# Layer 1's lookup tables in two float32r parts, in a kernel of four graph layers

## The chip, the cores and the metric

The kernel runs on one core of one Trainium2 chip. The metric is the device time of one execution in microseconds (us).

## The reference

The input is x with 16 graphs of 1,024 nodes and 128 features, and adj, one 1,024 x 1,024 matrix of zeros and ones for each graph. Four layers follow each other, each with a residual and a layer norm:

```python
x = layernorm(x + L0(x))   # attention over adj: q, k, v with relu, softmax over neighbours
x = layernorm(x + L1(x))   # max over neighbours
x = layernorm(x + L2(x))   # (x + adj^T x) through two dense layers
x = layernorm(x + L3(x))   # three SAGE convolutions on a dilated graph, batch norm, dense
```

The change is in layer 1:

```python
p = einsum('bnd,do->bno', x, W1 - W2)
q = einsum('bnd,do->bno', x, W2)
pre = p[:, :, None, :] + q[:, None, :, :] + b
return max(relu(pre) * adj[..., None], axis=2)
```

Layer 3 first thins out the graph ("dilation"). It goes row by row through a matrix: a row's neighbours are counted, a part of them is removed by rank, and removals also take the mirrored column, so that later rows see them.

## The kernel before

**Layer 1.** Relu is monotone, so what is needed is the max of q[j, o] over the neighbours j of each row i. Seven columns j make a group, 147 groups a graph. For a chunk of 21 groups, VectorE (DVE) builds the maxima of all 128 subsets of a group's columns for every o (`sub`, L257, seven instructions). For three groups at a time TensorE (PE) transposes them into PSUM (`pt`, L264) and ScalarE (ACT) copies them to `table` (L266). For each group PE multiplies `lit` with the columns of adj (`pm`, L271, bf16, one PSUM buffer of its own with the tag `subset`), and ACT makes of it the one-hot subset of each row (`hot`, L273, two buffers). A float32 product of `table` and `hot` (`pg`, L148 in the helper `product`) looks the maxima up, into one of two PSUM buffers with the tag `wide`, which other layers share. DVE takes the running max (`best`, L249). The product of group g is issued behind the `pm` of group g + 1.

**What runs beside it.** The function `between` is called after every group. It puts in the layer 2 of the graph before (`gin`), the layer 0 of the graph after (`attention`, one tile of 128 rows every ten groups) and an even share of the dilation (`dilation`, 1,400 pieces for 2,352 groups).

**The dilation** works on 8 blocks of 128 rows, for all 16 graphs. Each block loads its rows as bytes (`E`, L327, one buffer, by POOL's queue) and the block's own corner (`Dg`). For each graph, `E` is cleared of what earlier blocks removed (L341) and counted by ACT (`junk`, L343 and L347). Then 127 steps follow, each a chain of ten small DVE instructions on 16 partitions (L361 to L374). The corner is written out and read back into `E` (L378 and L379), ACT counts it (`junk`, L383, 16 times), seven small DVE instructions make constants of the counts, and for each graph DVE ranks (`rank`, L400, one buffer), ACT takes an absolute value (L401) and DVE makes `gone` (L403), which SP's queue stores.

**The order.** Instructions are not issued in the order in which the code lists them. A scheduler places them on each engine, by priorities and by its own estimate of how long each takes, and fixes the order when the program is built. Each engine then runs its own list in that order and waits where a semaphore is not yet set. A change in layer 1 can therefore move other work.

**Layer 3** starts when layers 0 to 2 are done (L486 is its first large DVE instruction) and is the same in both kernels.

Of the kernel before, what the change touches and what calls it, by code (L numbers as in the profile page):

```python
"""Four graph layers with residuals and layer norms, on one NeuronCore.  # L1

Rows of a graph's features stand either on the partitions (x[n, d]) or in the free dimension  # L3
(xT[d, n]); adj is read both as it is and with its rows and columns swapped, in bfloat16, in which
its zeros and ones are exact.

Layer 0  masked attention, a tile of 128 query rows at a time.
Layer 1  max over neighbours of q[j, o]: relu is monotone, so relu(p + b + max q) is the max of
         relu(p + q + b), and a row without neighbours gives 0. Seven columns j make a group; the
         maxima of its 128 subsets are tabled for every o, and a matrix product with the one-hot  # L10
         subset of each row i (exact) looks them up. What is left is a max over the 147 groups.
Layer 2  GIN; x is split in three bfloat16 parts, whose sum is x, for the product with adj.
Layer 3  GraphSAGE on the dilated graph. Dilation goes row by row: in a block of 128 rows only the
         block's own 128 columns change while it is worked on, so they alone are stepped through,
         for 16 graphs at once on 16 partitions; the removals of whole rows follow in bulk. It
         depends on adj and nodemask alone and is issued between the groups of layer 1.
"""

# [8 lines left out]

F32 = mybir.dt.float32
BF = mybir.dt.bfloat16
U8 = mybir.dt.uint8  # L30
AF = mybir.ActivationFunctionType
ALU = mybir.AluOpType
# [3 lines left out]
B, N, D, H2 = 16, 1024, 128, 256  # L36
# [14 lines left out]
def subset_tables():  # L51
    """lit[j, g, s]: 1 or -1 for a column j of group g, in subset s or not; 1 - |s|."""
    s = np.arange(P)
    lit = np.zeros((CH, GC, P), np.float32)
    for j in range(CH):
        lit[j, j // GS] = np.where((s >> (j % GS)) & 1, 1.0, -1.0)
    size = sum((s >> k) & 1 for k in range(GS))
    return lit, (1.0 - size).astype(np.float32).reshape(P, 1)
# [3 lines left out]
def tile_graph_layers(ctx: ExitStack, tc, a, out):  # L62
# [14 lines left out]

# [1 line left out]
    ident = consts.tile([P, P], F32, name="ident")  # L79
# [38 lines left out]

    # Half of the mask: [b, n] and [p, t, b]; the whole in the latter form.
    mask_u = consts.tile([B, N], U8, name="mask_u")  # L120
    nc.sync.dma_start(out=mask_u, in_=a["nodemask"])
    half_mask = consts.tile([B, N], F32, name="half_mask")
    nc.vector.tensor_scalar(half_mask, mask_u, 0.5, None, op0=ALU.mult)
    nm = consts.tile([P, T, B], F32, name="nm")
# [10 lines left out]

# [1 line left out]
    def transposed(dst, src):  # L137
        """dst[d, n] from src[p, t, d], n = t * 128 + p."""
        for h in range(2):
            p = bank("ptr")  # L140
            for t in range(4):
                nc.tensor.transpose(p[:, t * P:(t + 1) * P], src[:, 4 * h + t, :], ident)
            nc.scalar.copy(dst[:, halves[h]], p)

    def product(lhsT, rhs, name):
        p = wide(name)
        for s in halves:
            nc.tensor.matmul(p[:, s], lhsT, rhs[:, s], start=True, stop=True)  # L148
        return p
# [14 lines left out]
    def split(pool, src, left):  # L164
        """Three bfloat16 tiles, the sum of which is src."""
        parts = [pool.tile([P, T, D], BF, name=f"part{k}") for k in range(3)]
        for k in range(3):
            nc.scalar.copy(parts[k], left if k else src)  # L168
            if k < 2:
                nc.vector.tensor_sub(left, left if k else src, parts[k])  # L170
        return parts

    def aggregate(parts, m, name):
        """[d, i]: the sum over j of x[j, d] m[j, i]."""
        p = wide(name)
        for s in halves:
            for c in range(T):
                for k in range(3):
                    nc.tensor.matmul(p[:, s], parts[k][:, c, :], m[:, c, s],  # L179
                                     start=(c == 0 and k == 0), stop=(c == T - 1 and k == 2))  # L180
        return p

    def layers_012():
# [4 lines left out]

# [1 line left out]
        def attention(b, An):  # L190
# [14 lines left out]
            for t in range(T):  # L205
# [3 lines left out]
                e = w4.tile([P, N], F32, name="e", bufs=2)  # L209
                # scores of relu'd q and k are not negative, and the mask is 0 or 1.  # L210
                nc.vector.scalar_tensor_tensor(e, psc, CLAMP_HI, An[:, t, :], op0=ALU.min, op1=ALU.mult)
# [21 lines left out]

# [1 line left out]
        def max_conv(b, AT, between):  # L235
# [7 lines left out]

            def look_up(g, table, hot):
                pg = product(table, hot, "pg")
                if g == 0:
                    nc.vector.tensor_copy(best, pg)
                else:
                    nc.vector.tensor_max(best, best, pg)  # L249

            last = None
            for g0 in range(0, NG, TG):
# [6 lines left out]
                for g in range(g0, g0 + TG):  # L259
                    at = (g - g0) % 3  # L260
                    if at == 0:
                        pt = bank("pt")
                        for k in range(3):
                            nc.tensor.transpose(pt[:, k * P:(k + 1) * P], sub[:, g - g0 + k, :], ident)  # L264
                        table = w2.tile([P, 3, P], F32, name="table", bufs=3)
                        nc.scalar.copy(table.rearrange("s g o -> s (g o)"), pt[:, :3 * P])  # L266
                    c, r = divmod(g, GC)
                    rows = min(CH, N - c * CH)
                    pm = wide("pm", "subset", 1)
                    for s in halves:  # L270
                        nc.tensor.matmul(pm[:, s], lit[:rows, r, :], AT[:rows, c, s], start=True, stop=True)  # L271
                    hot = w2.tile([P, N], F32, name="hot", bufs=2)
                    nc.scalar.activation(hot, pm, AF.Relu, bias=one_less)  # L273
                    if last is not None:
                        look_up(*last)
                    last = g, table[:, at, :], hot
                    between(g)
# [12 lines left out]

# [1 line left out]
        def gin(b, An):  # L292
# [26 lines left out]

# [1 line left out]
        # h1 = sf + 1 with sf = ceil(num / 2); half = num / 2 + 1/4 where the row is masked in,  # L321
        # 0 elsewhere: num > 10 where half > 5.5, num > 1 where half > 1.
        def dilation():
            for k in range(T):
# [4 lines left out]
                nc.gpsimd.dma_start(out=Dg, in_=adj[:, own, own])  # L329
                # Neighbours before and after the block's own columns.  # L330
                counts = dil.tile([P, 2, B], F32, name="counts")
# [25 lines left out]
                for n in range(P - 1):  # L357
                    mine = Dg[:, n, :]
                    m = slice(k * P + n, k * P + n + 1)
                    rank1 = small.tile([B, P], F32, name="rank1")  # L360
                    nc.vector.tensor_tensor_scan(rank1, mine, mine, before[:, n:n + 1], op0=ALU.add, op1=ALU.max)  # L361
# [7 lines left out]
                    nc.vector.tensor_scalar(at2, at, 2.0, -1.0, op0=ALU.mult, op1=ALU.add)  # L369
                    hit = small.tile([B, P], F32, name="hit")  # L370
                    nc.vector.tensor_scalar(hit, rank1, at, every, op0=ALU.is_equal, op1=ALU.max)  # L371
# [3 lines left out]
                    yield  # L375
                # Rows as each was when its turn came; what each removed.
                Dd = dram.tile([B, P, P], U8, name=f"own{k}")
# [3 lines left out]
                for b in range(B):  # L381
                    junk = dil.tile([P, N], BF, name="junk", tag="gone", bufs=2)
                    nc.scalar.activation(junk, E[:, b, :], AF.Copy, accum_out=num[:, b:b + 1])  # L383
                    yield
                # |scale * rank - centre| == width: both multiples of sf, the whole row, or none of it.
                half = dil.tile([P, B], F32, name="half")
# [35 lines left out]

        # Between the groups of a graph's layer 1: the last graph's layer 2, the next one's
        # layer 0 and an even share of the dilation.
        dilate = dilation()
# [38 lines left out]

# [1 line left out]
    xpool = ctx.enter_context(tc.tile_pool(name="xpool", bufs=1))  # L466
# [9 lines left out]
    def dilated(b):  # L476
        """[j, i], the edge from i to j that is left; kept for the later convolutions."""
        gone = sb.tile([P, T, N], BF, name="gone_all", bufs=1)
# [12 lines left out]
    def sage(b, l, m, hT, parts, stats):  # L491
# [23 lines left out]
        inv = sb.tile([P, N], F32, name="inv", bufs=1)  # L515
        # max(sqrt(s), 1e-12) = sqrt(max(s, 1e-24))
        nc.vector.tensor_scalar_max(inv, pn, 1e-24)  # L517
# [22 lines left out]
    def add_hidden(b, l, hT):  # L540
        """x += mask * (h_l @ Wl_l), with bl once."""
        p = wide("pl").rearrange("p (t d) -> p t d", d=D)
# [67 lines left out]
```

## Time and profile before

| What | Value |
|---|---|
| median of 3 runs | 9,834.1 us (9,832.8 to 9,841.0) |
| span of the profiled execution, first to last instruction | 9,842.3 us; the profile gives no other time for it |
| PE, DVE, ACT, POOL busy, share of the span | 85%, 81%, 44%, 5% |
| lookups `pg` on PE (two passes for each float32 product) | 9,408 matmuls, 4,516.5 us busy |
| `best` on DVE | 2,336, 1,213 ns each |
| `hot` on ACT | 2,352, 1,112 ns each |
| last `best` starts / layer 3's L486 starts | 7,957.6 / 8,038.5 us |
| mean granted TensorE clock | 0.926 |

The busy shares are averages over stages with different limits. In a row of the groups stand the line, the engine, the operation, what it writes and reads, shapes and count; behind the first bar its busy time and the mean duration of one, behind the second the idle time of the engine just before it and what ended most of that. In a row of the timeline stand the start and the duration in us, the engine, the line and the operation, and in brackets the idle time before it and its releaser. Matmuls are pipelined: four passes that follow each other show 1.88 us, and the distance from start to start is what one costs.

### The profile page before, as it was taken

What the parts mean: (1) busy time and instruction counts of PE and PEld (TensorE: products, weight loads), DVE (VectorE), ACT (ScalarE), POOL (GpSimd) and SP (SyncE); (2) the same over time, 40 slices, a digit from 0 to 9 for tenths busy, and PEclk for the clock granted to TensorE, in tenths of its full rate; (3) what the DMA queues carried; (4) which work ended last, traced back from release to release, by engine and by line L of the source; (5) the groups of instructions that cost most, each with busy time, mean ns of one, the idle gap of its engine ahead of it and who ended that gap; (6) DMA issues with size and microseconds to landing.
All of it is one profiled execution on the core that took longest, in us unless ns stands there. A gap on an engine that the chain in (4) does not pass through costs nothing. (4 is left out here: it accounts for less than half of the span.)

```text
span 9842.3 us, 86106 instructions
## 1 busy us (share of the span) xinstructions
PE 8394.1 (85%) x28929; PEld 4159.1 (42%) x29032; DVE 7991.7 (81%) x17348; ACT 4296.9 (44%) x5170; POOL 499.6 (5%) x447
## 2 busy tenths in 40 slices
PE   8888988898888888888889898989898967678775
PEld 4444444444444444444444444444444433344333
DVE  5998699869986998699869986998699968845556
ACT  4445544554455445544554455445444532122221
POOL 0000000000000000000000000000000001011111
PEclk9999999999999999999999999999999988889886
DMA  3010201020102010201020102010200047733332
GB/s 47 1 22 19 34 1 22 18 37 1 22 17 40 1 22 16 44 1 22 15 47 1 22 12 52 1 22 10 50 5 9 8 139 208 200 116 137 115 129 87
DMA packets 317235, 435.16 MB, mean 44 GB/s; under 512 B 105445, under 2 KB 156792, under 8 KB 316662
## 3 DMA queue, kind: packets, MB, share of 16 engines
q1 hardware_dynamic: 219696, 295.75, 9.1%
q0 software_dynamic: 92560, 132.72, 8.7%
q8 instruction: 227, 3.72, 0.2%
q10 hardware_dynamic: 4534, 1.19, 0.1%
q14 instruction: 218, 1.79, 0.1%
HBM read 461.64 MB, written 119.54 MB: 59 GB/s over the span
## 5 line engine op out<-in xcount | busy, mean ns | idle before, releaser
L148 PE MATMUL pg<-hot,table 128*128 128x512 f32 x9408 | 4516.5, 604 | 140.4 <-DVE best L249 83.0
L273 ACT ACTIVATE hot<-pm,one_less 128x1024 f32<-128x1024 f32 x2352 | 2616.1, 1112 | 2435.5 <-PE pm L271 2162.5
L249 DVE TENSOR_TENSOR best<-best,pg 128x1024 f32<-128x1024 f32 x2336 | 2833.9, 1213 | 465.4 <-PE pg L148 458.5
L148 PEld LDWEIGHTS pg<-hot,table 128*128 128x128 f32 x9408 | 1735.6, 191 | 1795.6 <-issue 1187.8
L271 PE MATMUL pm<-AT,lit 126*128 126x512 bf16 x4704 | 1428.1, 384 | 247.2 <-ACT hot L273 175.4
L271 PEld LDWEIGHTS <-lit 126*128 126x128 bf16 x4704 | 460.3, 99 | 1224.5 <-issue 1200.1
L266 ACT COPY table<-pt 128x384 f32<-128x384 f32 x784 | 371.5, 476 | 772.5 <-PE pt L264 763.8
L264 PE MATMUL pt<-ident,sub 128*128 128x128 f32 x2352 | 414.3, 284 | 179.4 <-DVE sub L257 99.8
L179 PE MATMUL pagg<-m,part 128*128 128x512 bf16 x2231 | 518.4, 383 | 36.8 <-DVE inv L517 25.3
L264 PEld LDWEIGHTS pt<-ident,sub 128*128 128x128 f32 x2352 | 305.1, 146 | 487.1 <-issue 244.3
L361 DVE TENSOR_TENSOR_SCAN rank<-Dg,before 16x128 f32<-16x128 uint8 x1016 | 477.6, 470 | 26.6
L179 PEld LDWEIGHTS <-part 128*128 128x128 bf16 x3072 | 298.5, 99 | 394.5 <-issue 55.0
L374 DVE TENSOR_TENSOR Dg<-Dg,hit 16x127 uint8<-16x127 uint8 (+63 forms) x1016 | 441.4, 434 | 22.9
L257 DVE TENSOR_TENSOR sub<-sub,q 128x21 f32<-128x21 f32 (+6 forms) x784 | 431.6, 550 | 15.7 <-ACT q L239 11.3
L208 POOL TENSOR_SCALAR pen<-An 128x1024 f32<-128x1024 bf16 x128 | 133.8, 1045 | 4639.8 <-DVE e L212 3004.0
L372 DVE SCALAR_TENSOR_TENSOR hit<-rank,sc,hit 16x128 f32<-16x128 f32 x1016 | 342.5, 337 | 25.0
L544 PE MATMUL pl<-w_L_gnn_Wl,hT 128*128 128x128 f32 x768 | 201.0, 369 | 181.0 <-DVE x L547 119.4
L168 ACT CAST part<-left 128x1024 bf16<-128x1024 f32 x128 | 133.6, 1044 | 490.4 <-DVE left L170 490.4
L226 PE MATMUL pav<-v,eT 128*128 128x128 f32 x2048 | 332.5, 329 | 12.9 <-ACT eT L223 12.5
L371 DVE TENSOR_SCALAR hit<-rank,sc 16x128 f32<-16x128 f32 x1016 | 336.9, 332 | 0.0
L226 PEld LDWEIGHTS pav<-v,eT 128*128 128x128 f32 x2048 | 309.8, 239 | 54.2 <-ACT eT L223 52.0
L519 DVE RECIPROCAL inv<-inv 128x1024 f32<-128x1024 f32 x48 | 314.3, 6549 | 19.1 <-ACT inv L518 19.0
(163 smaller groups left out, 8299.1 us busy)
## 6 DMA issues: line engine op xcount, KB each, us to landing
m<-kept SPq DMA_DIRECT2D x32, 2048.0 KB, 9.3
An<-in_adj_dram POOLq DMA_DIRECT2D x16, 2048.0 KB, 14.0
removed<-gone SPq DMA_DIRECT2D x128, 256.0 KB, 2.0
m<-in_adjT_dram POOLq DMA_DIRECT2D x16, 2048.0 KB, 13.5
gone_all<-removed SPq DMA_DIRECT2D x16, 2048.0 KB, 9.7
kept<-m SPq DMA_DIRECT2D x16, 2048.0 KB, 14.1
AT<-in_adjT_dram POOLq DMA_DIRECT2D x16, 2016.0 KB, 14.5
hidden<-r SPq DMA_DIRECT2D x48, 512.0 KB, 3.8
```

What stands on the lines that cost most here:

```text
L148: nc.tensor.matmul(p[:, s], lhsT, rhs[:, s], start=True, stop=True)
L179: nc.tensor.matmul(p[:, s], parts[k][:, c, :], m[:, c, s], start=(c == 0 and k == 0), stop=(c == T - 1 and k == 2))
L226: nc.tensor.matmul(pav[:, :D], eT[:, c, :], v[:, c, :], start=(c == 0), stop=(c == T - 1))
L249: nc.vector.tensor_max(best, best, pg)
L257: nc.vector.tensor_max(sub[:, :, n:2 * n], sub[:, :, 0:n], qg[:, g0:g0 + TG, k:k + 1].to_broadcast([P, TG, n]))
L264: nc.tensor.transpose(pt[:, k * P:(k + 1) * P], sub[:, g - g0 + k, :], ident)
L266: nc.scalar.copy(table.rearrange("s g o -> s (g o)"), pt[:, :3 * P])
L271: nc.tensor.matmul(pm[:, s], lit[:rows, r, :], AT[:rows, c, s], start=True, stop=True)
L273: nc.scalar.activation(hot, pm, AF.Relu, bias=one_less)
L361: nc.vector.tensor_tensor_scan(rank1, mine, mine, before[:, n:n + 1], op0=ALU.add, op1=ALU.max)
L372: nc.vector.scalar_tensor_tensor(hit, rank1, at2, hit, op0=ALU.is_equal, op1=ALU.max)
L374: nc.vector.tensor_tensor(Dg[:, n + 1:, n], Dg[:, n + 1:, n], hit[:, n + 1:], op=ALU.is_gt)
```

## The change

Each table is split in two. `high` is the transposed table written by ACT as float32r; `whole` is a second ACT copy in float32; `low`, their difference, is made on POOL as float32r. `hot` is written as float32r. The lookup of a group is two products for each half of the rows, with `high` and with `low`, added up in the same PSUM buffer. `high` and `low` have two buffers, `whole` one; `table` had three. Apart from that the mask is loaded by POOL's queue straight into float32, where SP's queue loaded bytes, and the small tiles `rank1` and `hit` of the dilation have two buffers in place of three. Comments are left out, so line numbers shift by up to eight.

```diff
+F32R = mybir.dt.float32r
...
-    mask_u = consts.tile([B, N], U8, name="mask_u")
-    nc.sync.dma_start(out=mask_u, in_=a["nodemask"])
     half_mask = consts.tile([B, N], F32, name="half_mask")
-    nc.vector.tensor_scalar(half_mask, mask_u, 0.5, None, op0=ALU.mult)
+    nc.gpsimd.dma_start(out=half_mask, in_=a["nodemask"])
+    nc.vector.tensor_scalar(half_mask, half_mask, 0.5, None, op0=ALU.mult)
...
-            def look_up(g, table, hot):
-                pg = product(table, hot, "pg")
+            def look_up(g, parts, hot):
+                pg = wide("pg")
+                for s in halves:
+                    for k, part in enumerate(parts):
+                        nc.tensor.matmul(pg[:, s], part, hot[:, s], start=(k == 0), stop=(k == 1))
...
-                        table = w2.tile([P, 3, P], F32, name="table", bufs=3)
-                        nc.scalar.copy(table.rearrange("s g o -> s (g o)"), pt[:, :3 * P])
+                        high = w2.tile([P, 3 * P], F32R, name="high", bufs=2)
+                        nc.scalar.copy(high, pt[:, :3 * P])
+                        whole = w2.tile([P, 3 * P], F32, name="whole")
+                        nc.scalar.copy(whole, pt[:, :3 * P])
+                        low = w2.tile([P, 3 * P], F32R, name="low", bufs=2)
+                        nc.gpsimd.tensor_sub(low, whole, high.bitcast(F32))
...
-                    hot = w2.tile([P, N], F32, name="hot", bufs=2)
+                    hot = w2.tile([P, N], F32R, name="hot", bufs=2)
...
-                    last = g, table[:, at, :], hot
+                    last = g, [t[:, at * P:(at + 1) * P] for t in (high, low)], hot
...
-                    rank1 = small.tile([B, P], F32, name="rank1")
+                    rank1 = small.tile([B, P], F32, name="rank1", bufs=2)
...
-                    hit = small.tile([B, P], F32, name="hit")
+                    hit = small.tile([B, P], F32, name="hit", bufs=2)
```

## The prediction

> **What bounds the kernel now.** I read the busy table and the 40 slices first, then the groups, the timeline of a few groups of layer 1, and the busy time by windows.
>
> ```profile
> PE 8394.1 (85%) x28929; PEld 4159.1 (42%) x29032; DVE 7991.7 (81%) x17348; ACT 4296.9 (44%) x5170; POOL 499.6 (5%) x447
> PE   8888988898888888888889898989898967678775
> DVE  5998699869986998699869986998699968845556
> ```
>
> TensorE looks like the bound. But VectorE (DVE) swings in a pattern of four slices, one block of the dilation, and stands at 9 in half of them. Layers 0 to 2 fill 33 slices; layer 3 isn't touched by the change.
>
> ```profile
> L148 PE MATMUL pg<-hot,table 128*128 128x512 f32 x9408 | 4516.5, 604 | 140.4 <-DVE best L249 83.0
> L273 ACT ACTIVATE hot<-pm,one_less 128x1024 f32<-128x1024 f32 x2352 | 2616.1, 1112 | 2435.5 <-PE pm L271 2162.5
> L249 DVE TENSOR_TENSOR best<-best,pg 128x1024 f32<-128x1024 f32 x2336 | 2833.9, 1213 | 465.4 <-PE pg L148 458.5
> ```
>
> A lookup (one group) is 4 passes of PE in `pg`, 1.11 us of ACT in `hot`, 1.21 us of DVE in `best`. DVE has waited only 459 us for `pg` in all. The timeline of a stretch without dilation shows the cadence of a group:
>
> ```profile
> 2010.69 0.60 PE L271 MATMUL pm<-AT,lit 126*128 126x512 bf16 x2
> 2011.12 1.88 PE L148 MATMUL pg<-hot,table 128*128 128x512 f32 x4
> 2011.38 1.11 ACT L273 ACTIVATE hot<-pm,one_less 128x1024 f32<-128x1024 f32 x1 [1.04 <-PE pm L271]
> 2012.84 0.60 PE L271 MATMUL pm<-AT,lit 126*128 126x512 bf16 x2
> ```
>
> 2012.84 - 2010.69 = 2.15 us: four f32 passes of 0.427 and two bf16 passes of 0.214. Here PE is the bound. Elsewhere (columns: window, its length, PE, PEld, DVE, ACT, POOL busy, clock, DMA share, GB/s):
>
> ```profile
> 123.00:7995.00 7872.00, 7007.85 (x23082) 3407.84 (x23096) 6794.78 (x15779) 3842.24 (x4658) 267.02 (x269) 0.95 0.10 19
> 2091.00:2214.00 123.00, 119.57 (x412) 58.77 (x411) 91.40 (x202) 70.38 (x115) 3.92 (x4) 0.97 0.16 33
> 2214.00:2337.00 123.00, 109.96 (x365) 52.76 (x364) 118.47 (x291) 57.86 (x67) 4.22 (x4) 0.98 0.00 1
> ```
>
> With the dilation's steps in play DVE is busy 118.5 of 123 us, and the gaps between dependent steps take the rest: DVE is full. So both are bounds in turn, and a cheaper product pays only where DVE has slack. Adding along DVE's order the start-to-start distances that the same neighbours show where nothing waits gives 7,063 us up to the first instruction of layer 3 (L486), which starts at 8,038.5. DVE idles 975 us; that is all there is to win, and all later stalls are new.
>
> **What the skill says.** "FP8 and Floating Point Precision", TensorE Precision Notes: a true FP32 product takes four passes, reduced FP32 is read as 4 bytes and truncated. The trace agrees on the four (0.854 us per f32 product of 512 columns against 0.214 in bf16); no float32r is in it. "GPSIMD Engine Reference", Elementwise: a tensor_tensor of 2048 takes 4497 ns; L522 here takes 2.44 us for 1024. "SBUF — State Buffer", Who interferes with whom: a DVE instruction with two SBUF inputs and a GpSimd instruction that reads SBUF exclude each other, and the later one blocks for the whole instruction. The trace agrees:
>
> ```profile
> 626.84 1.04 POOL L208 TENSOR_SCALAR pen<-An 128x1024 f32<-128x1024 bf16 x1 [24.61 <-PE pz L148]
> 627.66 0.22 DVE L367 SCALAR_TENSOR_TENSOR sc<-sc 16x1 f32<-16x1 f32 x1
> 8212.51 3.16 DVE L486 TENSOR_TENSOR m<-m,gone_all 128x1024 bf16<-128x1024 bf16 x2
> 8212.67 2.44 POOL L522 TENSOR_TENSOR inv<-inv,mask 128x1024 f32<-128x1024 f32 x1 [31.10 <-DVE inv L519]
> ```
>
> L367 (mean 145 ns) takes 0.22 and ends with `pen`; two L486 (1.29 us elsewhere) take 3.16 behind L522.
>
> **The parts.**
>
> 1. Products. 9,408 passes of 0.427 become as many of 0.214, taking one pass for a float32r product (bounds: one and four passes). PE loses 2,352 x 0.854 = 2,009 us of work, 0.85 a group. Next late is the loop through the single `subset` buffer: 0.21 between the two `pm`, 0.41 to `hot`, 1.11, 0.05 back to `pm` = 1.79 us. It isn't changed.
>
> 2. ACT. `high` costs what `table` did; `whole` adds 784 x 0.476 = 373 us. Both stand before a `hot`, partly beside the 0.62 us of `pm`: +0.11 a group, so the loop is 1.90. PE's work for layers 0 and 2 (about 75 us a graph, 0.5 a group) stands in the same queue; I charge 0.3 of it: 2.2 us a group (bounds 1.9 and 2.4).
>
> 3. POOL. 784 `low`, each estimated at 0.8 us: the elements of L522 scaled (0.92), or the skill's row (0.84), the fastest L522 (2.11 us) giving 0.79. `low` must be there one group after its transposes; `high`, `whole`, `low` take 0.48 + 0.48 + 0.8, within a group's 2.2 plus the buffered lookups, so I put no wait on it. In POOL's queue it stands behind `pen`, `ln_rs` and the loads of `An`, `AT`, `E`, whose waits are for work that DVE's order has ahead of the lookup anyway. But it locks the port: in the before timeline a 0.8 us lock at a random moment meets a two-input DVE instruction in half the cases and costs 0.27 us in the mean, 784 x 0.27 = 210 us. Where DVE waits anyhow that is hidden: I take 80, bounds 0 and 230.
>
> 4. The mask's load moves from SP to POOL's queue with a cast, ahead of `An`. Its transposes stood at 4.3 us, `X` lands for the next at 17.1: covered; uncovered it would be some 10 us. `rank1` and `hit` with two buffers are DVE's alone: nothing.
>
> 5. The order. The built programs differ here most. Before, a dilation step is placed every group or two; in the changed program steps are rarer between lookups and each block's remainder comes last. 76 steps stand before lookup 147 in the old order, 52 in the new. In the first block the last step stands behind lookup 226 before and 294 after; the 16 scans (L400) then spread over 37 lookups before, over 3 after; the first `E` of the next block (L341) comes 25 lookups after the last `gone` before, none after. The other blocks repeat it. That takes three waits from under cover:
>
> ```profile
> 957.82 2.29 DVE L400 TENSOR_TENSOR_SCAN rank<-E 128x1024 f32<-128x1024 uint8 x1
> 960.20 1.24 ACT L401 ACTIVATE rank<-rank,centre,scale 128x1024 f32<-128x1024 f32 x1 [2.79 <-DVE rank L400]
> 961.48 1.28 DVE L403 SCALAR_TENSOR_TENSOR gone<-rank,width,E 128x1024 bf16<-128x1024 f32 x1
> 997.42 1.19 POOL L327 DMA_DIRECT2D E<-in_adj_dram  x1 [45.63 <-DVE share L228]
> ```
>
> DVE waits 1.35 us between each scan and `gone`, since `rank` has one buffer: 16 x 1.35 = 21. Ahead of it, `own` out and back (7.3 us) and 16 `junk` (L383, 1.04 apart) less one scan: 22. Behind it, the load of `E`, 26.0 us to landing: 27. The counts of the next block are then ACT's: 55 us against 43 of DVE, 12. Together 8 x 43 + 7 x 39 = 617 us. Most of DVE's old idle time goes; this takes its place. In return, 5,683 instead of 7,362 neighbours are two dependent dilation steps, each saving about 0.1 us: the same addition along the new order gives 6,904 to L486, 159 less.
>
> 6. Short stretches. Along the new order, runs of eight lookups hold on average less than 2.2 us of DVE work a lookup in 36% of the places; the shortfall sums to 332 us (123 at 1.9, 518 at 2.4).
>
> Sum of DVE's way to L486: 6,904 work + 617 blocks + 332 short stretches + 80 lock + 92 at the start (77 idle in the first 123 us, 15 in the lookups that follow without dilation) + 100 at the graphs' ends (8 x 9 + 7 x 4: `ln_rs`, `xT`, `pq`) + 10 before layer 3 = 8,135 against 8,038.5: +96. The profiled span is 9,842.3, so 9,939; it lies 8.2 above the median 9,834.1, and I put 9,930 for a median. The terms' bounds together (in squares: 209 and 186 for short stretches, 80 and 150 for the lock, about 115 for the blocks) give -260 and +265: own range 9,680 to 10,190.
>
> **Rivals.** (a) Faster: the loop holds 1.9 us and locks fall into waits: 6,904 + 617 + 123 + 202 = 7,846, -192, 9,642. It decides from short stretches below 236 us at the same lock. For it: PE and ACT have room (1.4 + 0.5 and 1.4 us a group). Against: PE's queue is in order and waits for `e` (166 us before L221). (b) No change: gains and stalls within 20 us. (c) The clock falls: PE's work drops to some 60% of the span, and the window from 7,995 to 8,118 us has a clock of 0.72 with PE busy for 64 of 123 us. With 2.4 us a group and the full lock: 8,135 + 186 + 150, 10,266. (d) The change isn't what it says: float32r takes the two double passes of before, or four single ones each. At 2.7 us a group the shortfall is some 800: 10,400; at four passes, 3.96 us a group on PE plus 0.5: 12,280.
>
> **The numbers.** My case of slower 0.52, (a) 0.23, (b) 0.10, (c) 0.10, (d) 0.05. The range 9,680 to 10,190 leaves out half of (a), half of (c) and (d). Faster by over 0.2% (20 us, about what a measurement of this kernel can tell) 0.23, same 0.10, slower 0.67.
>
> **What would show it.** Right: `pg` passes 0.214 apart; each block a stretch of some 130 us where PE is nearly idle; DVE waiting at `gone` for ACT about 1.4 us 100 times, at the first `E` of a block about 27 us seven times, at the block's first small instruction for `junk` about 20. Wrong: passes of 0.427; bursts in which DVE doesn't wait; two-input DVE instructions no longer than now; or DVE idle at `best` far from 330 us.

## The result, and the profile after

The changed kernel takes 10,017.0 us, the kernel before 9,834.5 us beside it: 1.0182 times as long, 95% interval 1.0167 to 1.0196. The profiled execution has a span of 10,017.0 us (before 9,842.3) and a mean granted TensorE clock of 0.856 (before 0.926). First the busy table of after and two of its rows of 40 slices:

```profile
PE 6938.9 (69%) x29032; PEld 4206.2 (42%) x29032; DVE 8181.0 (82%) x17348; ACT 4586.5 (46%) x5954; POOL 1307.7 (13%) x1232
...
PE   7786588647774787388738873888387816778775
...
DVE  6998699969996999699969996999699968845456
```

TensorE (PE) has lost 1,455 us of busy time. VectorE (DVE) has gained 189. In the PE row every block of the dilation now ends with a low digit (5, 4, 4, four times 3, 1): there the dilation's remainder holds DVE and PE runs out of work. The groups concerned (behind the first bar busy us and mean ns, behind the second idle us ahead of it):

```profile
L253 DVE TENSOR_TENSOR best<-best,pg 128x1024 f32<-128x1024 f32 x2336 | 2843.9, 1217 | 208.7 <-PE pg L249 194.1
L249 PE MATMUL pg<-hot,high 128*128 128x512 f32 x4704 | 2269.6, 488 | 164.8 <-DVE best L253 58.9
L249 PE MATMUL pg<-hot,low 128*128 128x512 f32 x4704 | 1905.7, 411 | 89.3 <-POOL low L274 89.0
L274 POOL TENSOR_TENSOR low<-whole,high 128x384 fp32r<-128x384 f32 x784 | 800.9, 1022 | 4513.7 <-ACT whole L272 4342.1
L369 DVE TENSOR_TENSOR_SCAN rank<-Dg,before 16x128 f32<-16x128 uint8 x1016 | 527.4, 519 | 20.0
```

`pg` is still 9,408 passes: a half's two products in float32r (the type in which the tables and `hot` are now written) are one record each, where its one float32 product was two records of 427 ns. Now they stand 234 ns apart in the median, from start to start in the trace. DVE waits for them only 209 us (before 465). But a step's scan takes 519 ns; it took 470 before:

```profile
L361 DVE TENSOR_TENSOR_SCAN rank<-Dg,before 16x128 f32<-16x128 uint8 x1016 | 477.6, 470 | 26.6
```

What else DVE waits for, from its waits (total us, times, longest us):

```profile
DVE best L253 <- PE pg L249: 194.1, 253, 4.3
DVE E L349 <- DMA E<-in_adj_dram: 180.9, 7, 26.6
DVE gone L411 <- ACT rank L409: 158.7, 121, 1.4
DVE half L395 <- ACT junk L391: 115.7, 8, 14.5
...
DVE rank L408 <- DMA E<-own: 59.3, 8, 8.0
```

The last four are the stalls at the end of each block. Before, `half` and `rank` waited 1 us at most in all, and these two were small:

```profile
DVE gone L403 <- ACT rank L401: 26.8, 44, 1.4
DVE E L341 <- PE pr L340: 21.8, 8, 5.3
```

Yet the sum tells another story. The busy time of the engines from the start to layer 3's first large DVE instruction (L486, in after L494), by windows (length; PE, PEld, DVE, ACT, POOL; clock, DMA share, GB/s), first of before, then of after:

```profile
0.00:8038.55 8038.55, 7097.97 (x23464) 3465.88 (x23481) 6849.61 (x15896) 3888.75 (x4737) 290.94 (x301) 0.95 0.11 21
```

```profile
0.00:8207.85 8207.85, 5621.31 (x23480) 3504.64 (x23481) 7044.60 (x15901) 4184.27 (x5527) 1098.96 (x1086) 0.86 0.11 21
```

Length less DVE's busy time is DVE's idle time: 1,188.9 us before, 1,163.3 after. So of the 169 us by which layer 3 starts later, busy time of DVE gives +195 and its idle time -26. The same DVE instructions take longer; the new stalls are there, but waits elsewhere have shrunk by as much. Adding up all durations, the two-input instructions of the dilation's steps grew most. The timeline of after shows how:

```profile
351.26 1.01 POOL L274 TENSOR_TENSOR low<-whole,high 128x384 fp32r<-128x384 f32 x1 [0.59 <-ACT whole L272]
...
351.45 0.83 DVE L375 SCALAR_TENSOR_TENSOR sc<-sc 16x1 f32<-16x1 f32 x1
```

L375 works on one element per partition. Here it starts 0.19 us into a `low` and takes 0.83: it ends when `low` ends. Its mean, before (as L367) and after:

```profile
L367 DVE SCALAR_TENSOR_TENSOR sc<-sc 16x1 f32<-16x1 f32 x1016 | 147.5, 145 | 25.9
```

```profile
L375 DVE SCALAR_TENSOR_TENSOR sc<-sc 16x1 f32<-16x1 f32 x1016 | 207.0, 204 | 18.9
```

This is no single case. In the trace of after 169 of the 2,032 instructions at L375 and L376 begin during a `low`; 155 of them end within 0.06 us of its end. Of the maxima 119 begin during a `low`, and they take no longer (13 ns in the mean).

### The profile page after: what moved, and what is told of

Its sections match the earlier page's. It is cut to its first block, busy times and chain, and to the rows that moved or that the text cites. A ratio compares the mean times of both kernels' runs of the same rounds, so it can differ in the third digit from the quotient of the medians.

```text
span 10017.0 us, 88548 instructions
## 1 busy us (share of the span) xinstructions
PE 6938.9 (69%) x29032; PEld 4206.2 (42%) x29032; DVE 8181.0 (82%) x17348; ACT 4586.5 (46%) x5954; POOL 1307.7 (13%) x1232
## 5 line engine op out<-in xcount | busy, mean ns | idle before, releaser
L281 ACT ACTIVATE hot<-pm,one_less 128x1024 fp32r<-128x1024 f32 x2352 | 2623.9, 1116 | 1897.8 <-PE pm L279 1644.4
L249 PE MATMUL pg<-hot,high 128*128 128x512 f32 x4704 | 2269.6, 488 | 164.8 <-DVE best L253 58.9
L279 PE MATMUL pm<-AT,lit 126*128 126x512 bf16 x4704 | 1445.1, 388 | 833.0 <-ACT hot L281 740.1
L249 PE MATMUL pg<-hot,low 128*128 128x512 f32 x4704 | 1905.7, 411 | 89.3 <-POOL low L274 89.0
L274 POOL TENSOR_TENSOR low<-whole,high 128x384 fp32r<-128x384 f32 x784 | 800.9, 1022 | 4513.7 <-ACT whole L272 4342.1
L249 PEld LDWEIGHTS pg<-hot,high 128*128 128x128 f32 x4704 | 911.9, 196 | 635.4 <-DVE best L253 140.7
L249 PEld LDWEIGHTS pg<-hot,low 128*128 128x128 f32 x4704 | 926.2, 197 | 317.2 <-POOL low L274 154.4
L348 PE MATMUL pr<-ident_b,rp 128*128 128x128 bf16 x448 | 54.5, 250 | 950.6 <-DVE E L349 498.5
L270 ACT CAST high<-pt 128x384 fp32r<-128x384 f32 x784 | 373.9, 477 | 545.0 <-PE pt L268 463.4
L369 DVE TENSOR_TENSOR_SCAN rank<-Dg,before 16x128 f32<-16x128 uint8 x1016 | 527.4, 519 | 20.0
L272 ACT COPY whole<-pt 128x384 f32<-128x384 f32 x784 | 382.9, 488 | 67.0 <-POOL low L274 65.5
```

The source lines that it names most:

```text
L249: nc.tensor.matmul(pg[:, s], part, hot[:, s], start=(k == 0), stop=(k == 1))
L272: nc.scalar.copy(whole, pt[:, :3 * P])
L274: nc.gpsimd.tensor_sub(low, whole, high.bitcast(F32))
```

## The experiments

All were compared with the kernel before on their own chip (9,837 to 9,846 us there). "To layer 3", DVE busy and idle are from windows as above; the clock is that of the whole span. All of these come from the one profiled execution, whose time lies up to 32 us from the median (pe_sub2; order lies 26 below it, order_no_sub 25 above).

| Kernel | us | ratio to before, 95% | to layer 3 | DVE busy | DVE idle | clock |
|---|---|---|---|---|---|---|
| before | 9,841 | 1 | 8,038.6 | 6,849.6 | 1,188.9 | 0.926 |
| after | 10,017 | 1.0182 (1.0167 to 1.0196) | 8,207.9 | 7,044.6 | 1,163.3 | 0.856 |
| before_sub | 10,043 | 1.0206 (1.0190 to 1.0221) | 8,222.3 | 7,035.9 | 1,186.5 | 0.923 |
| no_sub | 9,875 | 1.0033 (1.0022 to 1.0045) | 8,069.6 | 6,785.3 | 1,284.3 | 0.852 |
| order | 10,056 | 1.0214 (1.0199 to 1.0230) | 8,228.7 | 7,038.4 | 1,190.3 | 0.877 |
| order_fine | 10,118 | 1.0286 (1.0271 to 1.0302) | 8,308.2 | 7,087.9 | 1,220.4 | 0.871 |
| order_no_sub | 9,807 | 0.9969 (0.9960 to 0.9978) | 8,013.0 | 6,805.1 | 1,207.9 | 0.871 |
| one_part | 10,238 | 1.0408 (1.0393 to 1.0424) | 8,445.0 | 7,008.9 | 1,436.2 | 0.800 |
| order_no_sub_one | 9,914 | 1.0075 (1.0058 to 1.0092) | 8,103.3 | 6,783.0 | 1,320.3 | 0.778 |
| three | 9,918 | 1.0070 (1.0053 to 1.0086) | 8,125.9 | 7,028.7 | 1,097.3 | 0.890 |
| order_no_sub_three | 9,739 | 0.9890 (0.9876 to 0.9905) | 7,931.9 | 6,796.6 | 1,135.3 | 0.911 |
| order_no_sub_four | 10,026 | 1.0183 (1.0168 to 1.0198) | 8,224.4 | 6,878.9 | 1,345.6 | 0.929 |
| pinned_three | 10,096 | 1.0259 (1.0245 to 1.0273) | 8,287.8 | 6,832.8 | 1,455.0 | 0.900 |
| pe_sub2 | 9,798 | 0.9954 (0.9939 to 0.9969) | 7,952.6 | 6,777.6 | 1,175.0 | 0.888 |

The theory at the start: two costs that add, GpSimd's (POOL) subtractions, which hold up DVE, and the stalls that the new order lays bare. The rivals: the lower clock, or one cost alone.

### The subtractions: put into before, taken out of after

before_sub adds to before nothing but a subtraction for each three groups (and `rank1` and `hit` with two buffers, as after has them, to make room):

```diff
                         nc.scalar.copy(table.rearrange("s g o -> s (g o)"), pt[:, :3 * P])
+                        spare = w2.tile([P, 3, P], F32, name="spare")
+                        nc.gpsimd.tensor_sub(spare, table, table)
```

> Before with one GpSimd subtraction of 128x384 for each three groups, of a table from itself into a tile that nobody reads; its float32 product and VectorE's order are before's (127 steps at lookup 294). Theory (the shared port): VectorE's two-input instructions grow as in after, 230 to 340 us of busy time, and the time rises to 10,060 to 10,170 us. If VectorE's idle time before the maxima (465 us) takes part of it up, 9,940 to 10,060. Rival 'durations grow with the clock or the order, not with GpSimd': 9,834 within 30 us, the subtractions lie beside other work.

10,043 us, 202 us slower: inside the range of the second case, 9,940 to 10,060, but not by its mechanism, for no wait took anything up. DVE's order is that of before, its wait for `pg` (451 us, before 459) and the clock nearly so; its busy time rises by 186 us (230 to 340 expected) and its idle time stays. Nobody waits for `spare`, and yet its whole effect is on the path. The window to layer 3 and two groups of before_sub:

```profile
0.00:8222.34 8222.34, 7179.71 (x23464) 3468.73 (x23481) 7035.89 (x15896) 3880.54 (x4737) 989.17 (x1085) 0.94 0.11 20
```

```profile
L268 POOL TENSOR_TENSOR spare<-table 128x384 f32<-128x384 f32 x784 | 697.6, 890 | 5402.3 <-ACT table L266 5352.4
...
L363 DVE TENSOR_TENSOR_SCAN rank<-Dg,before 16x128 f32<-16x128 uint8 x1016 | 503.0, 495 | 26.6
```

no_sub takes the subtraction out of after and leaves the number of ScalarE (ACT) copies as it is and the order close to after's (104 scans are followed at once by their removal, 106 in after); the order was not held fixed:

```diff
-                        whole = w2.tile([P, 3 * P], F32, name="whole")
-                        nc.scalar.copy(whole, pt[:, :3 * P])
                         low = w2.tile([P, 3 * P], F32R, name="low", bufs=2)
-                        nc.gpsimd.tensor_sub(low, whole, high.bitcast(F32))
+                        nc.scalar.copy(low, pt[:, :3 * P])
```

> After without GpSimd's 784 subtractions: low is a second rounded copy by ScalarE from PSUM, and the unrounded copy is gone, so the subtraction is left out and the table's second part is wrong; products, waits on ScalarE and the order of VectorE's stream are after's (117 steps at lookup 294, 104 scans followed at once by their removal). Theory (the shared port): VectorE's instructions with two SBUF inputs return to before's durations (step product 147 ns, scan 478, Dg 441), 230 to 320 us of busy time, and the block stalls stay at 500 to 560: 9,690 to 9,790 us. Rival 'the longer durations are the lower clock's or a new neighbourhood's': durations stay at 207, 527 and 483 ns, and the time within 40 us of after's 10,017.

9,875 us, 142 us faster than after. Less DVE time than hoped for reached the end: 9,690 to 9,790 were expected. The durations and the block stalls are as expected. These are one group and the window to layer 3 of no_sub:

```profile
L367 DVE TENSOR_TENSOR_SCAN rank<-Dg,before 16x128 f32<-16x128 uint8 x1016 | 475.6, 468 | 18.5
```

```profile
0.00:8069.57 8069.57, 5572.09 (x23461) 3567.45 (x23481) 6785.27 (x15900) 4172.26 (x5527) 295.12 (x302) 0.86 0.11 22
```

The scan is back at 468 ns though the clock is 0.852 and the order is nearly after's, so these don't make it longer. DVE's busy time falls by 259 us, of which 121 come back as idle time: a DVE that is done sooner waits longer for `pg` (344 us at `best` in place of 209). The price of the subtractions on the path is thus 202 us in before's stream and 142 in after's (there it also holds what PE's 89 us of waiting for `low` cost). What is left is 34 us over before: in this order, with the subtraction's cost out of the way, halving the product gains nothing.

### The order, steered

order keeps after's arithmetic and places each maximum behind the last dilation instruction that was issued four groups before it (an edge that fixes the order and waits for nothing). order_no_sub has both edits.

```diff
-                    nc.vector.tensor_max(best, best, pg)
+                    behind(nc.vector.tensor_max(best, best, pg))
...
+            def behind(it):
+                if len(marks) > 4 and marks[-4] is not None:
+                    tc.add_manual_dep(it.ins, marks[-4].ins.name, mybir.DependencyInfo(
+                        mybir.DependencyClass.NoSync, mybir.DependencyReason.DATA), reason="order")
...
+                marks.append(mark[0])    # the dilation's last Dg or gone
```

> After with its arithmetic unchanged and the order of VectorE's stream steered: each maximum is placed behind the dilation instruction that was emitted four groups earlier. The steps per lookup become those of before (127 at lookup 294, after has 115), the last step of block 0 stands at lookup 240 (after 294), and a row's scan is followed at once by its removal 3 times (after 106). Theory of two costs (order, and GpSimd's subtractions): VectorE's idle time at the block stalls (E 205, gone 159, half 116, rank 63 us, 543 in all) falls to some 60; of the idle time before the maxima, and of the gain from independent neighbours, some 100 to 150 us come back as a loss. So the span falls by 330 to 440: 9,580 to 9,690 us. Rival 'all of the loss is GpSimd's and the clock's': within 40 us of after, 9,980 to 10,060. Rival 'the order is worth only what the two columns of steps differ, the stall moves to the E load alone': 9,820 to 9,860.

> Both at once: the second part is a rounded copy by ScalarE (the subtraction is left out) and the maxima are placed as in the kernel with the steered order. If order and port are two costs that add, the sum of the two single gains: 9,270 to 9,450 us. Rival 'one hides the other' (what the port no longer takes is found as a wait on TensorE or ScalarE): not below the better of the two single ones by more than 60 us, some 9,580 to 9,650.

The theory of two costs missed order by some 400 us; 10,056 lies in the range of its rival 'all of the loss is GpSimd's and the clock's'. order_no_sub at 9,807 lies in neither range. The stalls did go: `E` and `gone` wait 62 and 32 us, `half` and `rank` under 2 each. The time did not: 38 us slower than after (31 by the two ratios to before), and DVE's idle time is 1,190 us where it was 1,163. It has moved into many short waits, at `best` (298 us), at layer 0's and layer 2's instructions. From TensorE's waits in order:

```profile
PE pm L285 <- ACT hot L287: 952.6, 1353, 6.7
PE pg L250 <- DVE best L254: 310.4, 356, 4.0
```

In after these were 740.1 and 58.9 us. ACT's wait at `hot` for `pg` rises with them, from 246.8 to 1,091.9 us. The waits fit this account, which was not tested by itself: a maximum behind a whole step lets go of its PSUM buffer later, so PE stops, then ACT, then DVE. So the steering does not only take stalls away, it also makes waits of its own. Without the subtraction it gains 69 us (9,875 to 9,807); with it, it loses 38. In the steered pair the subtraction costs 249 us. Here `low` itself takes 1,156 ns in the mean (1,022 in after). In the trace 97 `low` take more than 1.2 us; 93 of these begin while a two-input DVE instruction runs, 55 of them during a scan of L414, and end 0.8 us behind it in the median. So each side blocks the other.

Was the steering too coarse? order_fine places each maximum behind as many dilation instructions as stand ahead of it in before:

```diff
+AHEAD = list(accumulate(zlib.decompress(base64.b64decode(...))))
...
-                    nc.vector.tensor_max(best, best, pg)
+                    it, n = nc.vector.tensor_max(best, best, pg), min(next(ahead), len(issued))
+                    if n:
+                        tc.add_manual_dep(it.ins, issued[n - 1].ins.name, ...)
```

> After with its arithmetic unchanged and VectorE's stream led closer to before's: each maximum is placed behind as many dilation instructions as stand ahead of it in before (before's own counts, as a list), not behind a whole step. 9 dilation instructions at a stretch between two maxima come 169 times (350 in the kernel steered by steps, 18 in before); 127 steps at lookup 294, 12 scans followed at once by their removal. Theory 'the coarse steering lost what it saved': idle time before the maxima falls from 298 us to some 230 with the block stalls still gone, 9,930 to 9,990 us. Rival 'VectorE's idle time is handed on whatever the order' (it was 1,162 us in after, 1,189 in the steered kernel and 1,188 in before): the sum stays at 1,150 to 1,220 us and the time at 9,995 to 10,060.

Slower again, 10,118 us. The theory of the coarse steering falls: leading after's stream closer to before's does not bring before's time, and the idle time before the maxima is 308 us, not 230. Neither time was met. DVE's idle time as a whole, 1,220 us, is what the rival said. It grew by 30 us over order and busy time by 50.

### Fewer and more passes

one_part leaves out the product with `high` and order_no_sub_one does the same to order_no_sub:

```diff
-                    for k, part in enumerate(parts):
-                        nc.tensor.matmul(pg[:, s], part, hot[:, s], start=(k == 0), stop=(k == 1))
+                    for k, part in enumerate(parts[1:]):
+                        nc.tensor.matmul(pg[:, s], part, hot[:, s], start=(k == 0), stop=(k == 0))
```

> After with the product of the first part left out: low alone is looked up, 4,704 of the 9,408 passes are gone (2,270 us of TensorE), everything else is issued as before, so the values are wrong. Theory 'the products are off the path in after': the loop is set by VectorE's own 7,045 us, the block stalls and the port, so no more than the 209 us before the maxima can move, and part of them come back: 9,960 to 10,020 us. Rival 'TensorE still sets the end through the 209 us and through the pieces of the other layers that stand behind the products': 9,780 to 9,900.

> The kernel with steered order and a second part copied by ScalarE (subtraction left out), and the first part's product left out as well: no port, no block stalls, half of the passes. Theory 'what is left of idle time on VectorE comes from TensorE's turn in the chain literals, one-hot, product': idle time falls from 1,207 us by 80 to 200, 9,610 to 9,730 us. Rival 'it comes from waits on ScalarE and on the pieces of the other layers': 9,760 to 9,830.

Both are slower than with two passes, by 221 and 107 us, and neither side had expected that. The clock falls to 0.800 and 0.778 and DVE's idle time grows. That suggested that a PE with less to do is granted less clock and gives back what it saved. If so, useless passes should help:

```diff
                 for s in halves:
+                    for _ in range(1):      # 2 in order_no_sub_four
+                        nc.tensor.matmul(pg[:, s], parts[0], hot[:, s], start=True, stop=True)
                     for k, part in enumerate(parts):
```

> After itself with the product of high issued twice, the first result overwritten; GpSimd's subtractions and all values as in after. VectorE's stream shifts half way to before's (127 steps and 5 scans at lookup 294, 52 scans followed at once by their removal, after 106). Theory 'clock and order': the granted clock rises from 0.856 to 0.88 to 0.90 and the block stalls halve, 9,940 to 10,020 us although TensorE does 1,010 us more. Rival 'each pass costs its time': 10,080 to 10,200 us. Rival 'only the port counts': as before with the added subtractions, 10,020 to 10,060 us.

> The kernel with steered order and without the subtraction (which is left out), with a third pass for each half: the product of high is issued twice and the first result is overwritten. TensorE gets 4,704 passes more, an estimate of 1,010 us at 0.214 us, that nobody needs; VectorE's order at the marks is the same (127 steps at lookup 294). Theory 'TensorE's granted clock falls with its own idle time, so work taken from it is partly given back' (0.778 with one pass at 9,914 us, 0.871 with two at 9,807 us): the clock rises to 0.89 to 0.92, VectorE's idle time stays at or under 1,207 us, 9,750 to 9,815 us. Rival 'a pass costs its time in the waits of the maxima, the clock is a mere record': 9,870 to 9,960 us.

> The same with the product of high issued three times, four passes for each half, as many as the float32 product of before takes; the subtraction is left out. VectorE's stream comes out like before's (last step of block 0 at lookup 222, before 226). Theory 'clock': 0.92 to 0.93 as in before, idle time near before's 1,188 us; a little above the three-pass kernel because the waits of the maxima return (465 us in before): 9,800 to 9,870 us, which is before's own time. Rival 'each pass costs': 9,930 to 10,080 us.

They do help, by a little more than the theory said: after gets 99 us faster with 4,704 passes more, order_no_sub 68 us. With a fourth pass it turns: 10,026 us, inside the range of the rival 'each pass costs', and the theory's 9,800 to 9,870 was missed. And the extra passes also make the scheduler draw up another order. So pinned_three is order_no_sub_three with every instruction of DVE and, the extra passes apart, of PE held in the order of order_no_sub (POOL's stream comes out the same, ACT's differs in 346 of 5,506 places):

```diff
+    for engine, code in (("DVE", DVE), ("PE", PE)):    # order_no_sub's streams
...
+        for n in places:
+            for i in (follow.get(kept[n].name), kept[n]):    # an extra pass ahead of its own
+                if i is not None:
+                    if last is not None:
+                        behind(i, last)
+                    last = i
```

> The three-pass kernel (second product of high issued first and overwritten, subtraction left out) with every instruction of VectorE, of GpSimd and, the extra passes apart, of TensorE in the order of the two-pass kernel with steered order; ScalarE's stream differs in 346 of 5,506 places. It answers whether the useless passes gained 68 us (9,807 to 9,739) by the clock or by the finer order that the scheduler made around them. Theory 'clock': granted clock 0.90 to 0.92, 9,730 to 9,780 us. Rival 'order': the passes then only cost, 9,800 us or more; from 9,830 they cost even net of the clock.

10,096 us. With the order of these engines held, the passes cost 289 us (9,807 to 10,096), although the clock rises from 0.871 to 0.900. The clock theory falls as an account of the gain; its rival "order" stands. The same instructions in the order that the scheduler makes when it counts the third pass take 9,739 us, 357 us less. The group of the maxima, first of order_no_sub_three, then of pinned_three:

```profile
L256 DVE TENSOR_TENSOR best<-best,pg 128x1024 f32<-128x1024 f32 x2336 | 2893.4, 1239 | 315.0 <-PE pg L252 302.6
```

```profile
L306 DVE TENSOR_TENSOR best<-best,pg 128x1024 f32<-128x1024 f32 x2336 | 2899.8, 1241 | 542.7 <-PE pg L302 525.6
```

From the first to the second DVE waits 228 us longer for the products, and ACT's wait at `hot` for `pg` to release a buffer rises from 460 to 1,142 us. What differs in the built streams: in 606 of 2,352 lookups of order_no_sub and pinned_three PE takes the literals (`pm`) of the group two later ahead of a product, in 293 of order_no_sub_three, 247 of after, 158 of before. A product so placed waits for the next `hot` first. This count goes with the waits in this pair, but it was not varied by itself, and it does not order the times: order_no_sub takes 9,807 us with its 606, order_no_sub_four 10,026 with 137. What in the order is worth the 357 us is open. The kernel that would close the case, two passes in the order of order_no_sub_three, was not run. Nor were one_part and order_no_sub_one with the order held: how much of their 221 and 107 us is order and how much clock is open.

### The whole computation without GpSimd

pe_sub2 forms the rest on PE, into a second bank, and ACT writes it to `low` (`minus` is the identity times -1). No `whole`, no subtraction:

```diff
+                        rest = bank("rest")
+                        for k in range(3):
+                            r = rest[:, k * P:(k + 1) * P]
+                            nc.tensor.matmul(r, sub[:, g - g0 + k, :], ident, start=True, stop=False)
+                            nc.tensor.matmul(r, minus, high[:, k * P:(k + 1) * P], start=False, stop=True)
+                        low = w2.tile([P, 3 * P], F32R, name="low", bufs=2)
+                        nc.scalar.copy(low, rest[:, :3 * P])
```

> The whole computation without GpSimd: the rest is formed by TensorE, as sub times identity plus high times minus identity into a second bank, and ScalarE copies it into low. 784 times three more float32 products of 128 columns and three float32r ones, an estimate of 1.2 to 1.5 us for each triple from the 0.30 us of pt's transposes: 940 to 1,180 us more of TensorE, so its busy time is near before's 8,000. VectorE's order comes out close to before's (127 steps at lookup 294, 4 scans followed at once by their removal). Theory 'port and order decide': no port, no stalls, idle before the maxima up to before's 465 us at most: 9,790 to 9,880 us. Rival 'the longer chain from pt to low delays every third product': 9,900 to 10,050.

9,798 us, in the range of 'port and order decide': 0.9954 of before (0.9939 to 0.9969), 219 us under after, the fastest here that leaves out nothing. Two of its groups, DVE's scan and its wait for the products:

```profile
L255 DVE TENSOR_TENSOR best<-best,pg 128x1024 f32<-128x1024 f32 x2336 | 2831.3, 1212 | 368.5 <-PE pg L251 353.8 <-DVE sc L379 0.4 <-PE pt L270 0.3
...
L374 DVE TENSOR_TENSOR_SCAN rank<-Dg,before 16x128 f32<-16x128 uint8 x1016 | 476.3, 469 | 22.5
```

DVE's busy time is 6,778 us, the lowest of all, and its idle time 1,175 is no worse than before's. The four lines of the block stalls hold 121 us, where after has 543. PE does more work than in after (7,756 us against 6,939) and the kernel is faster. It changes both the subtractions and the order, so how the 219 us divide between the two it does not show.

## Why the prediction was right, and where it was not

The direction was right and the time inside the range, 87 us over the forecast of 9,930; 62 of these are the lock, put at 80 us and worth 142. By its steps:

1. **Products: right.** One pass each; 234 ns apart at the lower clock. Rival (d) is out.
2. **ACT: right in size.** `whole` takes 383 us (373 forecast), and no row shows DVE waiting for it.
3. **POOL: the term that was mis-sized.** `low` takes 1.02 us, not 0.8, and PE waits 89 us for it where I put no wait. The lock was set at 210 us uncovered, with 130 hidden "where DVE waits anyhow": 80 left. Set after beside no_sub: the subtractions add 259 us to DVE's busy time, 121 of these are taken out of its idle time, and 142 us are left on the time. So the cover was near the forecast in this order, and the lock itself was too small; 210 us scaled by 1.02 / 0.8 would be an estimate of 268. Such cover is not sure: in before_sub, where DVE waits 451 us for `pg`, none of it helped, idle time stayed at 1,186 us and 202 us arrived in full. The Trainium skill's "SBUF — State Buffer", Who interferes with whom, which the step rested on, agrees with the traces: the scan, `Dg` and L375 with two SBUF inputs grow and shrink with POOL's instruction, while `best`, with one input in PSUM, stays at 1,213 to 1,219 ns in before, before_sub, after and no_sub.
4. **Mask: right.** The first lookup's copy to `best` starts at 114.5 us (before 117.5).
5. **Order: the stalls were right, their price was not.** Forecast 8 x 21 at `gone`, 7 x 27 at `E`, 8 x 22 ahead of the scans: 168, 189 and 176 us; measured 159, 181 and 175. With the counts, 617 were forecast and 543 stand at these four lines. But their sum is not what they cost: order takes 446 us of them away, makes other waits, and is no faster. The gain from fewer dependent neighbours was forecast too high: the overlap of DVE's instructions (sum of durations less busy time) grows by 130 us in after, but only by 78 in no_sub, where no subtraction lengthens them; 159 were forecast, counting gaps too.
6. **Short stretches: right without the lock.** 209 us stand at `best` in after, and "far from 330" was to be a sign of being wrong. But in no_sub it is 344: what is missing in after went to cover the lock, as step 3 had it.

Without its 80 us of lock the sum forecast +16 us, and no_sub measures +34. That this part came out near is luck. To layer 3, DVE's busy time in no_sub is only 64 us under before's, where 159 less work was forecast (that figure counts the gaps between dependent instructions too). And its idle time rises by 95 us, where the waits were to rise by 176 (617 + 332 + 92 + 100 + 10 = 1,151 against 975). Two errors of opposite sign cancel. The 1,151 us can't be set against after's idle time of 1,163, which also holds those gaps; in before they are 213 us (7,063 less 6,850). Two slips in the sums change nothing: the loop of step 1 adds up to 1.78 us, and the lower bound in squares is 252, not 260.

**The rivals.** (c) named a fact: the clock in the loop fell from 0.95 to 0.87. But it does not order the times: 0.923 stands with 10,043 us and 0.852 with 9,875. (a) needed short stretches below 236 us, which stand in after (209) and not in no_sub (344); "at the same lock" did not come true. (b) is near what no_sub shows: 34 us over before once the subtractions are gone.

## What to carry to other kernels

Ahead of giving GpSimd work "because it is idle", look at what VectorE runs meanwhile: where VectorE is the full engine and its instructions have two SBUF inputs, 784 subtractions that nobody waits for cost 202 us. A wait elsewhere may hide a part of that or nothing: 121 of 259 us in one order, none in the other. Do not book a stall at its length: compare the engine's whole idle time, since an order that took 446 us of stalls away left it at 1,190. And where a scheduler fixes the order from its own estimates, a cheaper instruction is a new order as well; hold the order fixed before saying what an instruction costs, for the same work differed by 357 us between two orders.

## What was not expected of the hardware

The estimate of the lock counted instructions with two inputs. Some with one tensor input grew beside POOL's too: `hit` from 332 to 370 ns (363 in before_sub) and the normalisation of X (L161, in after L162) from 337 to 389 (363); both are back at 330 in no_sub. `hit` before and after:

```profile
L371 DVE TENSOR_SCALAR hit<-rank,sc 16x128 f32<-16x128 f32 x1016 | 336.9, 332 | 0.0
```

```profile
L379 DVE TENSOR_SCALAR hit<-rank,sc 16x128 f32<-16x128 f32 x1016 | 375.9, 370 | 0.0
```

A subtraction of 384 elements per partition that writes float32r (`low`) takes 1,022 ns in the mean and 1,011 in the median; one that writes float32 (`spare`) takes 890 and 826. `spare` also reads one tile twice, so which difference does it is open.

The mean granted clock of after and of the kernels made from it goes with the number of passes on PE: 0.778 and 0.800 with one pass a half, 0.852 to 0.877 with two (0.888 in pe_sub2, whose PE has more to do besides), 0.890 to 0.911 with three, 0.929 with four.
